# Eight pauses of GpSimd between gathers removed, and three transfers moved from SyncE's queue to ScalarE's, in a two-layer graph kernel

## The chip, the cores and the metric

The kernel runs on one core of a Trainium2 chip. The metric is device time in microseconds, the median of several runs; lower is better. One further execution was taken with the hardware profiler, and all stages, waits and durations below are of that execution, in microseconds from its start.

## The reference

```python
h = maximum(layernorm(x), 0)                       # x: 4096 x 512, adj: 4096 x 4096, all f32
d = rowsum(adj) ** -0.5                            # 0 where the row sum is 0
x = x + relu((d[:, None] * adj * d[None, :]) @ h @ W0 + b0)      # layer 0

h = maximum(layernorm(x), 0)                       # layer 1
s, t = (h @ W1) @ a[:512], (h @ W1) @ a[512:]
e = leaky_relu(s + t.T, 0.2)                       # 4096 x 4096
p = softmax(where(adj > 0, e, -1e12), axis=1)
q = -softmax(where(adj > 0, -e, -1e12), axis=1)
x = x + elu(concat([p @ h, q @ h], axis=1) @ wtrans)
```

About 0.8% of the entries of adj are nonzero (a symmetric random mask with the diagonal).

## The kernel before

Layer 0 is dense: TensorE multiplies the whole adj with the normalized rows. While it runs, the kernel finds, for every block of 64 output rows, which nodes are neighbours of any of them, and writes index lists. Layer 1 is sparse: for each pair of blocks it gathers the rows of h that the pair needs from a table in HBM and works on those alone.

**Tables.** A row of a table holds 512 numbers of h, the score t (column `ROW_T`), and the mask bits of the output rows that the table serves. There are eight tables, each for eight blocks, that is four pairs. `table[4]` (`tab0` = 4) is filled first. Most rows of the other tables are written in layer 0; the last two groups of rows (512 and 256 rows, `GROUPS[-2:]`) are copied from `table[4]` during layer 1 by `copy_rows` (L1350 to L1355, two DMAs of 1032 and 516 KB per table). Table 5, the next one, is copied after the second product of layer 1 in program order, the others every six blocks.

**Gathers.** `gather` (L453 to L464) issues indirect DMAs from GpSimd's queue, one for each list of 128 nodes. A pair has 22 of them in three tiles of 8, 6 and 8 (`CHUNKS`), called a = 0, 1, 2. The first block of a pair uses tiles 0 and 1, the second block tiles 1 and 2, so each block has 14. `gather0` does this for pair 16, whose work is woven into the end of layer 0; `gather1` for pairs 17 to 31 and 0 to 15. The tiles of a pair have one buffer for even and one for odd places k in the order of pairs (`g_pools[k % 2, a]`), so a gather can start when the product two pairs earlier has read its buffer.

**Pauses.** `pause` (L447) is a GpSimd copy of one column of the last gathered part of a tile into a small tile `mark`. GpSimd executes in order, so the gathers behind it are issued only when that tile has landed. There are eight: one in `gather0`, and seven in `gather1`, for (k, a) = (0, 1), (1, 0), and a = 2 with k from 1 to 5. The scheduler of the framework places instructions of an engine by their expected readiness, except those that `tc.keep_in_program_order` ties to each other; the early pauses stand two gathers after the tile that they wait for.

**One block r of layer 1.** `weights(r)`: on VectorE the scores z = s + t (L469) and the slope step (L475), on ScalarE two exponentials, of z and -z (L479), on VectorE two masks for each gathered tile (L488) and a tree of sums (L493 to L499). For the first four blocks, r = 34 to 37 (`first`), scores, exponentials and masks are done for each gathered tile by itself. `product(r)`: 14 matrix products on TensorE (28 records, L1306), then the reciprocal `rl` of the sums (a matmul `cs`, L504, and L506 on VectorE) and the scaling of u to `us` on ScalarE (L1315). `turn(r)`: four transposes (`tp`, L514) and copies to `ut` on ScalarE (L518). `finish1(j)`, for a pair: 8 products with `wt_sb` (16 records, L1329), the elu and the store. The text calls a block's product r34, its tiles p34, z34, us34, and so on. Pair n holds blocks 2n and 2n + 1; g1_18 is tile a = 1 of pair 18.

The loop over blocks is a pipeline: behind product(r) stand the gathers for the pair two further on, the weights of block r + 2 and the turn of block r - 1.

**Transfers by SyncE.** At the start of layer 1, SyncE's queue holds two loads of s, then `wt_sb` (wtrans, 2048 KB), then after the second product the two copies to table 5; after that the loads and stores of the finished pairs.

Of the kernel before, what the change touches and what calls it, by code (L numbers as in the profile page):

```python
# [11 lines left out]
I32 = mybir.dt.int32  # L12
# [7 lines left out]
P = 128  # L20
# [239 lines left out]
def gcn_gat_kernel(  # L260
# [23 lines left out]
    nc = tc.nc  # L284
# [33 lines left out]
    with sbuf(name="init", bufs=1) as init:  # L318
        column = init.tile([P, P], F32, name="column")
        nc.vector.memset(column[:, 0:1], 0.0)  # L320
        n = 1
# [38 lines left out]
    def rows_of(g, e):  # L360
        return table[g][e * ER : e * ER + EN, :].rearrange("(k p) c -> p k c", p=P)
# [80 lines left out]
    def put_row(queue, g, j, h):  # L442
        return queue.dma_start(  # L443
            out=rows_of(g, j // EJ)[:, j % EJ, :ROW_W], in_=h.bitcast(I32)
        )

    def pause(pool, gt):  # L447

        mark = pool.tile([P, 1], I32, tag="mark", name="mark", bufs=1)
        i = nc.gpsimd.tensor_copy(mark, gt[:, gt.shape[1] - 1, 0:1])  # L450
        tc.keep_in_program_order(i)

    def gather(gt, n, a):  # L453

        c = sum(CHUNKS[:a])
        for k in range(CHUNKS[a]):
            nc.gpsimd.indirect_dma_start(  # L457
                out=gt[:, k, :],
                out_offset=None,
                in_=table[2 * n // RPT],  # L460
                in_offset=bass.IndirectOffsetOnAxis(
                    ap=idx[n // NH][:, n % NH, c + k : c + k + 1], axis=0
                ),
            )  # L464

    def scores(s, z, t):

        n = z.shape[1]
        return nc.vector.tensor_tensor(  # L469
            z, t.to_broadcast([P, n, RB]), s.unsqueeze(1).to_broadcast([P, n, RB]), ALU.add  # L470
        )

    def exps(z, p, bound=False, pin=False):

        nc.vector.scalar_tensor_tensor(z, z, ALPHA, z, ALU.mult, ALU.max)  # L475
        if bound:
            nc.vector.tensor_scalar(z, z, 2 * MAXS, -2 * MAXS, ALU.min, ALU.max)
        for g in range(2):
            i = nc.scalar.activation(p[:, :, g, :], z, AF.Exp, scale=(1.0, -1.0)[g])  # L479
            if pin:  # L480
                tc.keep_in_program_order(i)

    def mask_out(r, p, mask):

        m = mask[:, :, r % RPT * RB : (r % RPT + 1) * RB]
        for g in range(2):
            e = p[:, :, g, :]
            nc.vector.scalar_tensor_tensor(e, m, 0.0, e, ALU.is_gt, ALU.mult)  # L488

    def tree(pool, r, q, half, tag="tree", bufs=3):  # L490

        t = pool.tile([P, half, 2 * RB], F32, tag=tag, name=f"tree{r}", bufs=1)
        nc.vector.tensor_tensor(t, q[:, :half], q[:, half : 2 * half], ALU.add)  # L493
        while half > 2:
            n = half // 2
            nc.vector.tensor_tensor(t[:, :n], t[:, :n], t[:, half - n : half], ALU.add)
            half -= n
        total = pool.tile([P, 2 * RB], F32, tag="total", name=f"total{r}", bufs=bufs)
        nc.vector.tensor_tensor(total, t[:, 0], t[:, 1], ALU.add)  # L499
        return total  # L500
# [22 lines left out]
    with sbuf(name="y0", bufs=1) as y_pool, sbuf(name="wa", bufs=1) as wa_pool, sbuf(name="bits", bufs=4) as bits_pool, sbuf(name="small0", bufs=4) as small, ExitStack() as rest, ExitStack() as lists:  # L523
# [403 lines left out]
        i0, n = GROUPS[0]  # L927
        with sbuf(name="w0", bufs=1) as w0_pool, sbuf(name="ain", bufs=9) as ain, sbuf(name="xs", bufs=5) as x_pool, sbuf(name="at6", bufs=5) as at_pool, sbuf(name="bits6", bufs=3) as bits6, sbuf(name="ln", bufs=3) as ln_pool:
# [3 lines left out]
            for g in range(2):  # L932
                nc.gpsimd.dma_start(
                    out=lst_dram[g].rearrange("(p n) o -> p (n o)", p=P), in_=dummy
# [4 lines left out]
            for g in range(NTAB):  # L939
                nc.gpsimd.dma_start(  # L940
                    out=table[g].rearrange("(e r) c -> e r c", r=ER)[:, EN, :], in_=zero[:NE]
# [3 lines left out]
                out=rows_of(tab0, late0 // EJ)[:, late0 % EJ : late0 % EJ + n_late, :],  # L945
                in_=zero.unsqueeze(1).to_broadcast([P, n_late, ROW]),
# [178 lines left out]
        with sbuf(name="work2", bufs=2) as work, sbuf(name="sums2", bufs=2) as sum_pool, sbuf(name="at2", bufs=4) as at_pool, sbuf(name="scratch", bufs=1) as scratch, sbuf(name="pair", bufs=1) as pair:  # L1125
            gts, ps0, totals, u0 = {}, {}, {}, {}
# [6 lines left out]
            def gather0(a):  # L1133
                if a < 2:
                    k = 1 - a
                    gt = y_pool.tile([P, Y_PARTS[k] * F], F32, tag=f"y{k}", name=f"g0_{a}")
                else:
                    gt = t_pool.tile([P, T_PARTS[0] * 3 * H], F32, tag="t0", name=f"g0_{a}")
                gt = gt[:, : CHUNKS[a] * ROW].bitcast(I32)
                gts[a] = gt.rearrange("p (k c) -> p k c", c=ROW)  # L1140
                gather(gts[a], PAIR0, a)
                if a == 2:
                    pause(small, gts[a])

            def parts0(r):
                a = r % 2
# [59 lines left out]
            def step(jp):  # L1206
# [19 lines left out]
            k = late0 % EJ  # L1226
            nc.gpsimd.dma_start(
                out=rows_of(tab0, late0 // EJ)[:, k : k + n_late, ROW_W:],
                in_=late_m[:, k : k + n_late].bitcast(I32),
# [14 lines left out]
    def sparse_layer1():  # L1244
        with ExitStack() as pools:

            def pool(name, bufs):
                return pools.enter_context(sbuf(name=name, bufs=bufs))
# [4 lines left out]
            tmp, small, p_pool = pool("tmp", 1), pool("small1", 2), pool("p", 3)  # L1253
# [3 lines left out]
            wt_sb = wt_pool.tile([P, 2 * FC, F], F32, name="wt_sb")  # L1257
# [3 lines left out]
            def load_s(k):  # L1261

                srow[k] = s_pool.tile([P, 4 * P], F32, tag="s", name=f"s{k}")
                return nc.sync.dma_start(
                    out=srow[k], in_=s_dram[4 * k * P : 4 * (k + 1) * P].partition_broadcast(P)
                )

            def gather1(n, a):
                k = pairs.index(n)
                gt = g_pools[k % 2, a].tile([P, CHUNKS[a], ROW], I32, tag="g", name=f"g{a}_{n}")  # L1270
                gather(gt, n, a)
                gath.setdefault(n, []).append(gt)
                if (k, a) in ((0, 1), (1, 0)) or a == 2 and 0 < k < 6:
                    pause(small, gt)

            def parts(r):

                t = gath[r // 2][r % 2 : r % 2 + 2]
                return (t[0], 0, t[0].shape[1]), (t[1], t[0].shape[1], t[1].shape[1])

            def weights(r):

                nk = sum(CHUNKS[r % 2 : r % 2 + 2])
                z = tmp.tile([P, nk, RB], F32, tag="z", name=f"z{r}", bufs=1)
                p = p_pool.tile([P, nk, 2, RB], F32, tag="p", name=f"p{r}")
                s = srow[r // 8][:, r % 8 * RB : (r % 8 + 1) * RB]
                for gt, k, n in parts(r):
                    scores(s, z[:, k : k + n], gt[:, :, ROW_T : ROW_T + 1].bitcast(F32))
                    if r in first:
                        exps(z[:, k : k + n], p[:, k : k + n])  # L1290
                        mask_out(r, p[:, k : k + n], gt[:, :, ROW_W:].bitcast(U8))
                if r not in first:
                    exps(z, p)
                    for gt, k, n in parts(r):
                        mask_out(r, p[:, k : k + n], gt[:, :, ROW_W:].bitcast(U8))
                wgt[r] = (p, tree(small, r, p.rearrange("p k g c -> p k (g c)"), nk // 2))
# [20 lines left out]
            def turn(r):  # L1317
                if r % 2 == 0:
                    uts[r // 2] = ut_pool.tile([P, 2, FC, P], F32, tag="ut", name=f"ut{r // 2}")
                turn_u(r, us.pop(r), uts[r // 2])  # L1320
# [26 lines left out]
            first = order[:4]  # L1347
            later = [*range(tab0 + 1, NTAB), *range(tab0)]

            def copy_rows(g, j, n):  # L1350

                r = j // EJ * ER + j % EJ * P
                return nc.sync.dma_start(
                    out=table[g][r : r + n * P, :ROW_W], in_=table[tab0][r : r + n * P, :ROW_W]
                )  # L1355

# [2 lines left out]
                tc.keep_in_program_order(load_s(wanted.pop(0)))  # L1359
            for a in range(3):  # L1360
                gather1(pairs[0], a)
            tc.keep_in_program_order(
                nc.sync.dma_start(out=wt_sb, in_=wtrans.rearrange("(c p) f -> p c f", p=P))
            )
            for a in range(3):
                gather1(pairs[1], a)
            weights(order[0])
            weights(order[1])
            for k, r in enumerate(order):
                product(r)  # L1370
                if k % 6 == 1 and k // 6 < len(later):
                    for j, n in GROUPS[-2:]:
                        tc.keep_in_program_order(copy_rows(later[k // 6], j, n))
                if k + 4 - k % 2 < len(order):
                    for a in ((0,), (1, 2))[k % 2]:
                        gather1(order[k + 4 - k % 2] // 2, a)
                if k + 2 < len(order):
                    weights(order[k + 2])
                    if wanted and order[k + 2] % 8 == 7:
                        load_s(wanted.pop(0))  # L1380
                if k:
                    turn(order[k - 1])
                if k == 2:
                    finish1(PAIR0)
                if k % 2 and k > 1:
                    finish1(order[k - 3] // 2)
            turn(order[-1])
            finish1(order[-1] // 2)

    sparse_layer1()  # L1390
    bad = nc.values_load(
        verdict[0:1, 0:1],
# [38 lines left out]
```

## Time and profile before

| | |
|---|---|
| timed runs, us | 2120.07, 2124.37, 2126.74 (median 2124.37) |
| profiled execution, us | 2135.61, its span 2133.8 |
| mean TensorE clock granted | 0.976 of full |
| busy share: PE, DVE, ACT, POOL | 94%, 53%, 24%, 43% |
| end of layer 0's products | about 1038 us |
| first gather of pair 17 | 1052.58 us |
| first product of pair 17 | 1083.57 us |

In the profile, PE is TensorE, PEld its weight loads, DVE VectorE, ACT ScalarE, POOL GpSimd, SP SyncE; SPq and ACTq are their DMA issues. A group's row names the line of the code, the engine, the operation, what it writes and reads, how often it occurs, its busy time and mean duration in ns, and the idle time of the engine just before it with the main releaser. "issue" is idle time for which the profile shows no releaser. A row of the timeline gives start, duration, engine, line, operation and in brackets the idle time before it. A GpSimd gather ends in the profile [...] not when its data have landed.

### The profile page before, as it was taken

The page shows a single profiled execution, that of the slowest core. Times are in us where ns is not written, and L with a number is a line of the kernel's source. Part 1 is how long each engine was busy: PE and PEld are TensorE (multiplying, and loading weights), DVE is VectorE, ACT ScalarE, POOL GpSimd, SP SyncE. Part 2 cuts the span into 40 slices and gives each one's busy share as a digit, 9 for nine tenths or more (in the row PEclk, how much of TensorE's full clock was granted, in tenths as well). Part 3 has the DMA queues.
Part 4 walks back from the last instruction along what each step waited for, and adds up shares of the span by engine and source line. Part 5 has one row for each costly group of instructions (what it writes and reads, how often), then busy time and mean ns, then how long its engine had stood idle before and what let it go on. Part 6 is the DMA issues. An engine that isn't in the chain of part 4 may idle for free.

```text
span 2133.8 us, 20055 instructions
## 1 busy us (share of the span) xinstructions
PE 2010.4 (94%) x6456; PEld 1184.6 (56%) x6456; DVE 1121.2 (53%) x2805; ACT 511.8 (24%) x876; POOL 923.9 (43%) x988
## 2 busy tenths in 40 slices
PE   6999999999898989899878998999999999999998
PEld 3444447888787768787434443444444444444443
DVE  5444526463896469835644435445445445445441
ACT  4645612223232310001111212122122122122120
POOL 2010001111123310322467667777777777677740
PEclk9999999999999999999989999999999999999999
DMA  9988918786977875556587778888888888887850
GB/s 372 372 309 320 365 47 281 266 305 199 344 241 251 260 258 172 169 167 199 164 284 238 241 227 265 262 281 243 276 254 272 248 276 246 239 247 235 239 168 21
DMA packets 188041, 524.12 MB, mean 246 GB/s; under 512 B 25235, under 2 KB 34419, under 8 KB 187926
## 3 DMA queue, kind: packets, MB, share of 16 engines
q0 software_dynamic: 71296, 275.22, 41.7%
q1 hardware_dynamic: 88480, 196.46, 27.1%
q10 hardware_dynamic: 28150, 51.07, 6.7%
q8 instruction: 52, 0.85, 0.2%
q14 instruction: 63, 0.52, 0.1%
HBM read 430.83 MB, written 102.92 MB: 250 GB/s over the span
## 4 chain that ended last, share of the span: by engine, by line
PE 47%; DVE 6%; DMA 4%; POOL 4%; issue 3%; ACT 1%; ACTq 1%; another core or an unknown queue 0%; DVEq 0%; SPq 0%; POOLq 0%
PE u L1306 30%; PE o L1329 10%; PE p L899 5%; POOL g L457 4%; DMA at<-in_adj_t 2%; DMA g<-table,idx 1%; DVE keys L393 1%; PE tp L514 1%; DVE lst L391 1%; DMA table<-h 1%; ACTq L443 1%; PE u L1182 1%; ACT m L722 1%; DVE p L488 0%
## 5 line engine op out<-in xcount | busy, mean ns | idle before, releaser
L457 POOL DMA_INDIRECT g<-table,idx x704 | 753.4, 1070 | 266.6 <-issue 197.6
L1306 PE MATMUL u<-g,p 128*128 128x512 f32 x1736 | 766.7, 598 | 14.9 <-DVE p L488 9.7
L1306 PEld LDWEIGHTS u<-g,p 128*128 128x128 f32 x1736 | 326.8, 191 | 405.5 <-issue 382.2
L469 DVE TENSOR_TENSOR z<-g,s 128x512 f32<-128x512 f32 (+1 forms) x124 | 77.4, 624 | 422.6 <-DMA g<-table,idx 376.0
L899 PE MATMUL p<-t,sums 128*128 128x256 f32 x832 | 249.7, 385 | 15.9 <-DVE sums L887 12.8
L899 PE MATMUL p<-y,sums 128*128 128x256 f32 x832 | 253.6, 387 | 6.3 <-DVE sums L889 5.5
L899 PE MATMUL p<-y,at 128*128 128x256 f32 x832 | 253.9, 387 | 3.9 <-DMA at<-in_adj_t 2.6
L1329 PE MATMUL o<-wt_sb,ut 128*128 128x512 f32 x512 | 230.5, 603 | 0.9 <-ACT ut L518 0.5
L479 ACT ACTIVATE p<-z 128x896 f32<-128x896 f32 (+2 forms) x136 | 116.1, 903 | 313.3 <-DVE z L475 156.7
L899 PEld LDWEIGHTS p<-t,sums 128*128 128x128 f32 x832 | 160.1, 193 | 39.5 <-DVE sums L887 14.0
L899 PEld LDWEIGHTS p<-y,sums 128*128 128x128 f32 x832 | 161.5, 194 | 31.1 <-DVE sums L889 6.3
L899 PEld LDWEIGHTS p<-y,at 128*128 128x128 f32 x832 | 160.1, 194 | 30.9 <-issue 3.4
L858 PE MATMUL acc<-y,at 128*128 128x512 f32 x384 | 174.9, 593 | 2.4 <-ACT y L708 2.4
L488 DVE SCALAR_TENSOR_TENSOR p<-g,p 128x384 f32<-128x384 uint8 (+1 forms) x256 | 143.6, 620 | 60.8 <-ACT p L479 30.4
L733 POOL DMA_DIRECT2D table<-m x71 | 54.3, 766 | 251.9 <-ACT m L722 146.6
L1329 PEld LDWEIGHTS o<-wt_sb,ut 128*128 128x128 f32 x512 | 96.7, 194 | 111.9 <-issue 111.0
L722 ACT ACTIVATE m<-at 128x1024 uint8<-128x1024 f32 (+1 forms) x110 | 105.0, 987 | 181.2 <-DMA at<-in_adj_t 140.2
L899 PE MATMUL p<-t,at 128*128 128x256 f32 x416 | 127.0, 388 | 18.8 <-DVE w L782 17.7
L685 PE MATMUL yp<-w_sb,hx_t 128*128 128x512 f32 x256 | 122.2, 623 | 18.1 <-ACT y L708 15.8
L1315 ACT ACTIVATE us<-u,rl 128x512 f32<-128x512 f32 x62 | 42.5, 686 | 389.4 <-issue 237.8
L858 PEld LDWEIGHTS acc<-y,at 128*128 128x128 f32 x384 | 70.5, 190 | 80.5 <-issue 76.9
L886 DVE TENSOR_TENSOR sums<-at 128x256 f32<-128x256 f32 x104 | 43.3, 416 | 136.4 <-PE p L899 67.3
(183 smaller groups left out, 1720.3 us busy)
## 6 DMA issues: line engine op xcount, KB each, us to landing
at<-in_adj_t SPq DMA_DIRECT2D x136, 512.0 KB
ar<-in_adj SPq DMA_DIRECT2D x128, 512.0 KB
table<-h ACTq DMA_DIRECT2D x182, 258.0 KB
table<-m POOLq DMA_DIRECT2D x55, 256.0 KB
at<-in_adj_t SPq DMA_DIRECT2D x32, 384.0 KB
g<-table,idx POOLq DMA_INDIRECT x704
xr<-in_x SPq DMA_DIRECT2D x32, 256.0 KB
x<-x1d SPq DMA_DIRECT2D x32, 256.0 KB
```

Source lines behind the costliest of these rows:

```text
L457: nc.gpsimd.indirect_dma_start(out=gt[:, k, :], out_offset=None, in_=table[2 * n // RPT], in_offset=bass.IndirectOffsetOnAxis(ap=idx[n // ...
L469: return nc.vector.tensor_tensor(z, t.to_broadcast([P, n, RB]), s.unsqueeze(1).to_broadcast([P, n, RB]), ALU.add)
L479: i = nc.scalar.activation(p[:, :, g, :], z, AF.Exp, scale=(1.0, -1.0)[g])
L488: nc.vector.scalar_tensor_tensor(e, m, 0.0, e, ALU.is_gt, ALU.mult)
L685: nc.tensor.matmul(yp, hx_t[j][:, c * P : (c + 1) * P], w0_sb[:, c, :], start=c == 0, stop=c == FC - 1,)
L722: nc.scalar.activation(m, at, AF.Sign)
L733: nc.gpsimd.dma_start(out=rows_of(t, e)[:, c:, ROW_W + (a - t * TT) * P // 4 : ROW_W + (b - t * TT) * P // 4], in_=masks[i0][:, c:, (a - i ...
L858: nc.tensor.matmul(a, at[:, 0, it * P : (it + 1) * P], y0[j], start=j == 0, stop=j == NJ - 1)
L886: op(t[:, 0], a[:, :, 0, 1], a[:, :, 1, 1], ALU.add)
L899: i = nc.tensor.matmul(out, left[:, x * P : (x + 1) * P], right, start=jp == 0 and first, stop=jp == NP - 1 and (final or not first),)
L1306: nc.tensor.matmul(u, p[:, k0 + k].rearrange("p g c -> p (g c)"), gt[:, k, :F].bitcast(F32), start=k0 + k == 0, stop=k0 + k == nk - 1,)
L1329: nc.tensor.matmul(po, ut[:, g, c, :], wt_sb[:, g * FC + c, :], start=g == 0 and c == 0, stop=g == 1 and c == FC - 1,)
```

## The change

The function `pause` and its eight calls go. The exponentials of the first four blocks are tied into the program's order (`pin=True`), so that what is tied behind them stays behind them. `wt_sb` is loaded from ScalarE's queue after the weights of the first two blocks, and the two copies to table 5 are issued from ScalarE's queue as well; all later copies stay with SyncE.

```diff
-    def pause(pool, gt):
-
-        mark = pool.tile([P, 1], I32, tag="mark", name="mark", bufs=1)
-        i = nc.gpsimd.tensor_copy(mark, gt[:, gt.shape[1] - 1, 0:1])
-        tc.keep_in_program_order(i)
...
                 gather(gts[a], PAIR0, a)
-                if a == 2:
-                    pause(small, gts[a])
...
                 gath.setdefault(n, []).append(gt)
-                if (k, a) in ((0, 1), (1, 0)) or a == 2 and 0 < k < 6:
-                    pause(small, gt)
...
                     if r in first:
-                        exps(z[:, k : k + n], p[:, k : k + n])
+                        exps(z[:, k : k + n], p[:, k : k + n], pin=True)
...
-            def copy_rows(g, j, n):
+            def copy_rows(queue, g, j, n):
...
-                return nc.sync.dma_start(
+                return queue.dma_start(
...
-            tc.keep_in_program_order(
-                nc.sync.dma_start(out=wt_sb, in_=wtrans.rearrange("(c p) f -> p c f", p=P))
-            )
             for a in range(3):
                 gather1(pairs[1], a)
             weights(order[0])
             weights(order[1])
+
+            tc.keep_in_program_order(
+                nc.scalar.dma_start(out=wt_sb, in_=wtrans.rearrange("(c p) f -> p c f", p=P))
+            )
             for k, r in enumerate(order):
                 product(r)
                 if k % 6 == 1 and k // 6 < len(later):
                     for j, n in GROUPS[-2:]:
-                        tc.keep_in_program_order(copy_rows(later[k // 6], j, n))
+                        queue = nc.scalar if k == 1 else nc.sync
+                        tc.keep_in_program_order(copy_rows(queue, later[k // 6], j, n))
```

In the program as built, the order of the instructions on TensorE is the same in both versions. On GpSimd only the eight copies are gone. On SyncE only the three transfers are gone. On ScalarE and VectorE the order changes around blocks 34 to 38: the load of `wt_sb` follows p35's exponentials; us34 now precedes p36's first exponentials; us35 and, behind it, the copies to table 5 precede p37's exponentials; on VectorE the masks of p36 and of p37 stand behind the scores of their block's second tile, and rl35 stands behind z37's second tile and ahead of the masks of p37.

## The prediction

> **What bounds the kernel now.** I read the page's groups first, then busy time by stage, then the waits of PE and POOL inside the stage that the change touches, then the instructions in order of time there.
>
> ```profile
> L457 POOL DMA_INDIRECT g<-table,idx x704 | 753.4, 1070 | 266.6 <-issue 197.6
> L1306 PE MATMUL u<-g,p 128*128 128x512 f32 x1736 | 766.7, 598 | 14.9 <-DVE p L488 9.7
> ```
>
> Busy time by stage (us from the span's start; length; busy PE, PEld, DVE, ACT, POOL; PE clock; DMA share; GB/s):
>
> ```profile
> 1083.57:1302.90 219.33, 203.00 (x503) 92.62 (x503) 101.62 (x190) 40.71 (x70) 155.21 (x148) 0.96 0.80 242
> 1323.00:2000.00 677.00, 677.00 (x1765) 313.03 (x1764) 333.26 (x617) 139.05 (x232) 496.12 (x466) 1.00 0.83 257
> ```
>
> From 1323 us on PE is never idle: layer 1 is then bound by TensorE, about 31.5 us for a pair of blocks. Only its first seven pairs (1083.57 to 1302.90) leave PE idle, 219.33 - 203.00 = 16.3 us. Whatever this change gains must come from there, or from the 9.7 us just before it. The waits in that stage (in total, times, longest):
>
> ```profile
> PE tp L514 <- ACT us L1315: 11.1, 3, 4.6
> PE tp L514 <- issue: 4.0, 2, 2.3
> POOL mark L450 <- DMA g<-table,idx: 19.0, 7, 5.2
> ```
>
> PE waits for `us`, ACT's scaling of u; `us` stands in order behind exponentials, and its factor `rl` behind a `z` on DVE. Both wait for gathered rows. POOL, which makes the gathers, is meanwhile never held by a buffer (0.3 us on PE in this stage, against 47.0 us, 32 times, from 1320 to 2000 us). So here the chain is POOL, landing, DVE, ACT, PE. One of the waits removed, in order of time on POOL:
>
> ```profile
> 1218.35 0.94 POOL L457 DMA_INDIRECT g<-table,idx  x1 [0.30 <-issue]
> 1224.48 0.69 POOL L450 COPY mark<-g 128x1 int32<-128x1 int32 x1 [5.19 <-DMA g<-table,idx]
> 1225.33 1.78 POOL L457 DMA_INDIRECT g<-table,idx  x1 [0.16 <-DVE z L469]
> ```
>
> POOL ends a gather at 1219.29 and begins the next at 1225.33, where the ordinary gap is 0.30.
>
> [...] from 1084 to 1088 us POOL's queue held 58.9% of the engines' time and SP's 44.9%. [...] here landing follows the end of issue by 3.2 to 5.5 us, and those are the values I use. [...] an output product (16 `o` matmuls) takes 7.03 us warm, but 9.06, 8.31 and 8.73 us after the three waits.
>
> **Part 1: eight pauses go.** The one in layer 0 frees 0.7 us, but six gathers later POOL stands at L1227 for a landing anyway (3.73 us): worth nothing. The other seven, each as the time from the end of the gather before to the start of the next less 0.30:
>
> 3.05 (at 1089.85), 2.79 (1101.90), 1.34 (1123.49), 1.25 (1155.80), 4.10 (1188.57), 5.74 (1224.48), 5.55 (1260.91): 23.8 us in all.
>
> So gathers come earlier by 5.8 us for pair 18's last tiles, 7.2 for pair 19's, 8.4 for pair 20's, 12.5 for pair 21's, 18.3 for pair 22's, 23.8 for pair 23's. No other work hides behind them on POOL. With no drain at the pause, the copy traffic may lengthen landings; from 1262 us on gathers already run without pauses at a DMA share of 0.83, and landings stay covered.
>
> **Part 2: wtrans and the first copies leave SP.** On SP they were issued at 1072.6 to 1077.3 and ran to about 1094, in the landing of the first pair's gathers. In windows of 4 us SP's queue took 75.3% of the engines from 1076 to 1080. The first pair's first gathers, issued by 1073.2, were used only at 1080.10, 6.9 us later instead of about 3.3:
>
> ```profile
> 1080.10 0.69 DVE L469 TENSOR_TENSOR z<-g,s 128x512 f32<-128x512 f32 x1 [4.23 <-DMA g<-table,idx]
> ```
>
> Moved away, this lands near 1076.6, and r34 (the first product, 1083.57) starts about 3.5 us earlier. SP has nothing queued behind the three transfers until 1156.71, so SP gains nothing else.
>
> On ACT three issues are added: 0.38 us for wt_sb, twice 0.61 (the median for such copies) for table 5; together 1.6 us, with slack. By the built program's order wt_sb follows p35's exponentials, so about 1096 us; its first use is the output product after r36, about 1124. The 3.7 MB of wt_sb and copies together took 21 us before, so 28 us for 2.1 MB covers it. The copies stand behind us35, hence behind rl35, which DVE now holds behind z37's second half (pair 18's last gather, landing 1117.7 to 1119): they go out near 1121. A later set of copies (1220.4) was through in under 10 us, so table 5 is ready at 1131 to 1136; POOL wants it for pair 20 at 1152.72 - 7.2 = 1145.5. The cover is about 10 us; beyond it each us would hold POOL.
>
> **Part 3: pinned exponentials change the order on DVE and ACT.** In the built program p36's masks for its first gathered tile now come after z36's second half, which waits for g1_18. That lands at 1112.5 - 5.8 + 2.2 (wt_sb's traffic, as the g1_17 landing took 5.5 us against 3.3) = 1108.9. After z, its slope step and two masks, r36 starts near 1111.4, against 1110.93 now. So the 3.5 us of part 2 are lost again. In return us35 is no longer behind p37's exponentials: the stall at 1123 (4.58 us, then 2.03 us of cold `o`) goes, and r37 ends near 1143.3 instead of 1149.7, 6.4 earlier.
>
> **The sum.** After r37 PE again follows gathers, now pair 20's: rl37, rl38 and us38 wait for g0_20 and g1_20, earlier by 8.4 us, so r40 ends 8.4 to 9 us earlier. From pair 21 on the gathers lead PE by more each pair (12.5, 18.3, 23.8), and the later idle goes: 0.45 + 3.34 + 2.26 = 6.0 us, with 1.70 us of cold `o` and 0.6 at 1301. Total 8.7 + 8.3 = 17 us. From both sides: no more than all idle plus cold work, 16.3 + 5.0 + 2.4 (r34's cold start) + the 3.5, about 27; no less than 8 if landings lengthen by 3 us each and the later idle half stays. Behind, PE is full and nothing is won or lost.
>
> The profiled execution took 2135.61 us (span 2133.8), 11 more than the median of the timed runs, 2124.37. It has two stretches (1021 to 1028 and 1303 to 1323 us) where PE crawls with "issue" as the only cause, some 10 us that I take to be of that execution and leave as they are. Against its own time I expect 2118.6 us; carried to the median, **2107.4 us**.
>
> **Rivals.**
> - *Landings take the pauses' place* (15%). If the DMA engines set the pace, a freed POOL only makes a longer queue, and `z` waits as before. For: share 0.80 with PE idle, and 30 us of POOL work a pair (22 gathers of 1.06 us and gaps of 0.30) against 31.5 of PE leaves little. Against: 356 to 411 GB/s moved from 1076 to 1088, 242 on average. It gives 4 to 9 us, about 2118.
> - *The edit does nothing that counts* (7%): the stalls that go come back as waits of PE for `us` through DVE's order; 2122 to 2127.
> - *Slower: POOL is held by the copies* (10%). Table 5 is issued some 48 us later than now. If these copies need more than 24 us from 1121, because gathers no longer pause for them, pair 20's gathers stall. They lose the 7.2 us gained so far at 31 us and break even with the later pauses at about 24 + 18 = 42 us; at 55 us the loss is 13 us, 2137. Against: the 3.7 MB before took 21 us among gathers.
> - *All idle goes* (8%): 22 to 26 us, 2100.
>
> **How the numbers follow.** The likeliest case (60%) is 2107, by itself 2102 to 2114. To leave out no more than 2 in 10, the range runs from 2099 (all idle) to 2124. About 0.3%, 6.4 us, is what a measurement of this kernel can tell from no change. Faster: 0.60 + 0.08 + most of the first rival, 0.10, 0.78. Same: 0.05 + 0.07 = 0.12. Slower 0.10.
>
> **What would show it.** Right: no `mark` on POOL; gathers of pair 21 start about 12 us earlier against r34's start; `z` at about 1077 for the first pair; PE's waits for `us` under 4 us in the seven pairs; wt_sb and table 5 landed before their use; PE full from about 1200 us. Wrong: POOL waiting on "DMA table<-table" before pair 20; landings more than 6 us after issue through the stage; an `o` product waiting for wt_sb; or idle PE of 15 us or more in those pairs.

## The result and the profile after

| | before | after |
|---|---|---|
| timed runs, us | 2120.07 to 2126.74, median 2123.81 (4) | 2098.72 to 2107.48, median 2104.20 (4) |
| profiled execution, us (span) | 2135.61 (2133.8) | 2098.72 (2096.8) |
| first gather of pair 17, us | 1052.58 | 1049.76 |
| first product of pair 17 (r34), us | 1083.57 | 1078.52 |

The ratio is 0.9901 [0.9875, 0.9928]: 19.6 us faster at the median. The profiled executions differ by 37 us, nearly twice that. The one before was 12 us above its median and the one after is the lowest of its four, so the two traces may not simply be subtracted; the experiments below say what the surplus is.

The groups of the page after, the same two as before:

```profile
L451 POOL DMA_INDIRECT g<-table,idx x704 | 747.8, 1062 | 259.9 <-issue 186.4
L1296 PE MATMUL u<-g,p 128*128 128x512 f32 x1736 | 762.4, 596 | 9.8 <-DVE p L482 9.8
```

A gather costs POOL what it did (1062 ns against 1070): the time that went is not in the work. Busy time by stage after, in windows with the same meaning, from r34 on (us from the span's start; length; busy PE, PEld, DVE, ACT, POOL; PE clock; DMA share; GB/s):

```profile
1078.52:1287.71 209.19, 208.28 (x536) 95.97 (x537) 107.54 (x201) 43.62 (x75) 162.89 (x153) 0.99 0.88 281
1287.71:1965.00 677.29, 677.29 (x1769) 313.40 (x1768) 336.57 (x623) 139.73 (x235) 496.99 (x469) 1.00 0.84 259
```

PE is idle for 209.19 - 208.28 = 0.9 us where it was idle for 16.3. The DMA share rises from 0.80 to 0.88, as the same rows arrive in less time. The later window is full in both. PE's waits of the stage, all of them (total, times, longest), and what is left in front of the gathers:

```profile
PE u L1296 <- DVE p L482: 9.8, 2, 9.5
PE tp L508 <- ACT us L1305: 0.6, 1, 0.6
...
POOL g L451 <- issue: 45.4, 149, 0.3
```

The 11.1 us of waits for `us` are 0.6. Of the 9.8 us at the first line 9.5 stand ahead of r34, outside the window. On POOL every gap is the ordinary 0.30; no `mark` is left. The first pair's last scores, in order of time, and r34:

```profile
1075.05 0.69 DVE L463 TENSOR_TENSOR z<-g,s 128x512 f32<-128x512 f32 x1 [5.83 <-DMA g<-table,idx]
...
1078.52 1.22 PE L1296 MATMUL u<-g,p 128*128 128x512 f32 x1 [9.47 <-DVE p L482]
```

DVE now waits 5.83 us here instead of 4.23, yet ends earlier: a longer wait at one place can be the sign of work that came forward.

### The profile page after: what moved, and what is told of

Same layout as the page of the kernel before. It is cut to its first block, busy times and chain, and to the rows that moved or that the text cites. A ratio compares the mean times of both kernels' runs of the same rounds, so it can differ in the third digit from the quotient of the medians.

```text
span 2096.8 us, 20037 instructions
## 1 busy us (share of the span) xinstructions
PE 1996.2 (95%) x6456; PEld 1180.1 (56%) x6456; DVE 1120.1 (53%) x2805; ACT 511.3 (24%) x876; POOL 917.0 (44%) x980
## 3 DMA queue, kind: packets, MB, share of 16 engines
q1 hardware_dynamic: 86640, 192.78, 27.1%
## 4 chain that ended last, share of the span: by engine, by line
PE 49%; DVE 6%; DMA 5%; POOL 3%; issue 2%; ACTq 1%; ACT 0%; DVEq 0%; SPq 0%; POOLq 0%
PE u L1296 32%; PE o L1319 10%; PE p L893 5%; POOL g L451 3%; DMA g<-table,idx 2%; DVE keys L393 1%; PE tp L508 1%; DVE lst L391 1%; DMA table<-h 1%; DMA ld<-li,off 1%; DMA at<-in_adj_t 1%; PE u L1174 1%; ACTq L443 1%; DVE prod L816 0%; DMA table<-m 0%
## 5 line engine op out<-in xcount | busy, mean ns | idle before, releaser
L451 POOL DMA_INDIRECT g<-table,idx x704 | 747.8, 1062 | 259.9 <-issue 186.4
L463 DVE TENSOR_TENSOR z<-g,s 128x512 f32<-128x512 f32 (+1 forms) x124 | 77.5, 625 | 390.4 <-DMA g<-table,idx 357.8
L1319 PE MATMUL o<-wt_sb,ut 128*128 128x512 f32 x512 | 225.1, 592 | 0.5 <-ACT ut L512 0.5
L893 PEld LDWEIGHTS p<-t,sums 128*128 128x128 f32 x832 | 159.6, 193 | 37.5 <-DVE sums L881 15.5
L893 PEld LDWEIGHTS p<-y,sums 128*128 128x128 f32 x832 | 160.7, 193 | 29.9 <-DVE sums L883 7.3
L482 DVE SCALAR_TENSOR_TENSOR p<-g,p 128x384 f32<-128x384 uint8 (+1 forms) x256 | 143.2, 620 | 63.3 <-ACT p L473 62.3
L413 POOL DMA_INDIRECT ld<-li,off x48 | 43.2, 901 | 159.8 <-DMA ld<-li,off 115.8
```

Source lines behind the costliest of these rows:

```text
L413: return nc.gpsimd.indirect_dma_start(out=lst_dram[g][:, :], out_offset=bass.IndirectOffsetOnAxis(ap=off[g][:, e, c : c + 1], axis=0), in_ ...
L451: nc.gpsimd.indirect_dma_start(out=gt[:, k, :], out_offset=None, in_=table[2 * n // RPT], in_offset=bass.IndirectOffsetOnAxis(ap=idx[n // ...
L463: return nc.vector.tensor_tensor(z, t.to_broadcast([P, n, RB]), s.unsqueeze(1).to_broadcast([P, n, RB]), ALU.add)
L893: i = nc.tensor.matmul(out, left[:, x * P : (x + 1) * P], right, start=jp == 0 and first, stop=jp == NP - 1 and (final or not first),)
L1319: nc.tensor.matmul(po, ut[:, g, c, :], wt_sb[:, g * FC + c, :], start=g == 0 and c == 0, stop=g == 1 and c == FC - 1,)
```

## The experiments

**Theories.** A: the pauses give the whole gain; they kept gathers, and through `z`, `rl` and `us` the products, late. Rival: the gain comes with the transfers that leave SP. What stayed open after the first four runs was a second thing, called the crawl here: stretches in which PE executes one instruction in 0.7 to 2.8 us with no releaser. The traces before had them, the trace after had none.

All runs in one table. The ratio is to the kernel before, run between them on the same chip: e1 to e4 on one (2144.55 us), e5 to e8 on a second (2146.64), e9 to e11 on a third (2145.52), e12 on a fourth (2124.37). "r34" to "r46" are starts of products and "end" is PE's last instruction, each less the start of pair 17's first gather, worked out from the traces. "Issue" is PE's idle time without a named releaser from 1000 to 1350 us, and "crawl" what is left of it without the gaps that are waits, as told below the table. "us" are PE's waits for `us` or `ut` from r34 to 1350 us, the unnamed ones among them.

| run | us | ratio, interval | r34 | r36 | r37 | r40 | r46 | end | issue | crawl | us |
|---|---|---|---|---|---|---|---|---|---|---|---|
| before | 2123.81 | 1 | 31.0 | 58.4 | 85.0 | 144.0 | 250.3 | 1073.1 | 17.1 | 8.4 | 15.1 |
| after | 2104.20 | 0.9901 [0.9875, 0.9928] | 28.8 | 56.4 | 76.0 | 128.6 | 225.3 | 1039.0 | 0 | 0 | 0.6 |
| e1_pauses_gone | 2132.85 | 0.9945 [0.9931, 0.9960] | 30.9 | 58.1 | 100.5 | 152.4 | 249.1 | 1062.8 | 26.3 | 21.5 | 4.6 |
| e2_transfers_moved | 2141.83 | 0.9996 [0.9977, 1.0015] | 27.9 | 62.3 | 84.8 | 141.7 | 256.2 | 1073.5 | 27.4 | 9.3 | 12.1 |
| e3_early_pauses | 2136.96 | 0.9969 [0.9956, 0.9983] | 28.0 | 62.5 | 84.3 | 144.2 | 251.0 | 1064.7 | 27.1 | 13.8 | 5.9 |
| e4_late_pauses | 2140.72 | 0.9979 [0.9963, 0.9994] | 27.9 | 59.8 | 100.4 | 152.3 | 248.9 | 1066.4 | 30.6 | 21.5 | 0 |
| e5_after_again | 2132.36 | 0.9939 [0.9919, 0.9960] | 28.1 | 59.5 | 95.7 | 147.6 | 244.3 | 1059.9 | 27.1 | 19.2 | 0 |
| e6_tiles_placed | 2135.48 | 0.9950 [0.9931, 0.9969] | 27.9 | 56.1 | 99.1 | 151.0 | 254.4 | 1068.1 | 24.0 | 22.8 | 0.2 |
| e7_copies_later | 2140.68 | 0.9976 [0.9966, 0.9986] | 28.4 | 59.6 | 94.9 | 153.4 | 250.1 | 1068.5 | 28.2 | 23.4 | 0 |
| e8_before_again | 2150.61 | one run | 29.9 | 58.9 | 87.3 | 143.2 | 249.5 | 1076.6 | 25.9 | 13.1 | 16.3 |
| e9_tail_pauses | 2132.96 | 0.9946 [0.9924, 0.9968] | 28.3 | 59.4 | 96.5 | 148.4 | 245.1 | 1058.9 | 18.6 | 10.4 | 0 |
| e10_pauses_on | 2153.40 | 1.0038 [1.0025, 1.0051] | 30.3 | 58.7 | 86.5 | 142.5 | 250.7 | 1083.0 | 16.1 | 7.1 | 16.5 |
| e11_light_breaks | 2128.98 | 0.9926 [0.9901, 0.9952] | 27.9 | 60.9 | 82.2 | 149.1 | 245.8 | 1059.5 | 22.0 | 14.2 | 0 |
| e12_both_breaks | 2109.97 | 0.9931 [0.9917, 0.9944] | 28.7 | 57.9 | 77.5 | 132.2 | 228.9 | 1042.6 | 0 | 0 | 2.4 |

Not every gap without a named releaser is crawl. Two waits for `us` in the trace before, each with the row of ScalarE that made this `us`:

```profile
1127.07 0.69 ACT L1315 ACTIVATE us<-u,rl 128x512 f32<-128x512 f32 x1 [0.44 <-DVE rl L507]
1127.81 1.11 PE L514 MATMUL tp<-ident,us 128*128 128x128 f32 x4 [4.58 <-ACT us L1315]
...
1170.51 0.69 ACT L1315 ACTIVATE us<-u,rl 128x512 f32<-128x512 f32 x1 [9.80 <-DVE rl L507]
1171.25 0.66 PE L514 MATMUL tp<-ident,us 128*128 128x128 f32 x4 [1.74 <-issue]
```

Both times PE starts 0.74 us after `us` began, 0.05 us after it ended; the view names the releaser only once. A gap is counted here as a wait if a `us`, mask or sum that the instruction reads ended 50 to 60 ns before it, as at nearly all gaps with a named releaser (52 to 56 ns). Most of the long single gaps are such waits. So counted, the kernels with all the pauses of layer 1 (before, e2, e8, e10) have 12 to 17 us of waits for `us`, those with none of them 0 to 5. The 4.6 us of e1 lie inside a crawl and end 0.6 us after `ut`.

### e1: the pauses alone

The kernel before without `pause` and its calls; the transfers stay with SP, `exps` without `pin`.

```diff
-                if a == 2:
-                    pause(small, gts[a])
...
-                if (k, a) in ((0, 1), (1, 0)) or a == 2 and 0 < k < 6:
-                    pause(small, gt)
```

> The kernel before without the eight pauses; wtrans and the first copies stay on SyncE's queue, nothing is pinned. Theory A (PE is held by POOL's gathers in the first seven pairs, so the pauses cost the time): nearly the whole gain, 0.991 to 0.994 of before (13 to 19 us); r34 starts as late after the first gather of pair 17 as before (31 us), and PE waits under 5 us from there to pair 23. Rival B (the transfers in the first pair's landing cost the time, and POOL would be held by landings anyway): 0.998 to 1.001.

Measured 0.9945, just outside what theory A expected, and the same as the whole change on such a chip (e5, 0.9939; the intervals cover each other). The pauses give the gain.

### e2: the rest alone

The changed kernel with `pause` and all eight calls put back.

```diff
...
+                if (k, a) in ((0, 1), (1, 0)) or a == 2 and 0 < k < 6:
+                    pause(small, gt)
```

> The changed kernel with all eight pauses put back: only the pinned exponentials and the move of wtrans and the first copies to ScalarE's queue are left. Theory A: r34 starts 2 to 4 us earlier against the first gather of pair 17, but from r38 on PE follows the same paused gathers as before, so 0.997 to 1.001 of before. Rival B: most of the gain, 0.990 to 0.994.

Measured 0.9996 [0.9977, 1.0015]: no change, as theory A has it; the rival falls. The columns r34 and r36 show why. With the transfers on SP (before, e1, e8, e10) r34 starts 29.9 to 31.0 us after the first gather, in all others 27.9 to 28.8: the move does bring the first product forward by 2 us or so. At r36 the four stand at 58.1 to 58.9 and the others at 56.1 to 62.5, median 59.5: it is gone again. In e2 PE waits 6.3 us for masks ahead of r36, where the kernel before waits 4.58 us for `us` behind it. The run takes the moved transfers and the pinned order together; it does not separate the two.

### e3 and e4: which pauses

The changed kernel with four early pauses back (e3), or with the three late ones (e4). In the profile before, these cost POOL 3.05 + 2.79 + 1.34 + 1.25 = 8.4 us and 4.10 + 5.74 + 5.55 = 15.4 us.

```diff
...
+                if (k, a) in ((0, 1), (1, 0), (1, 2), (2, 2)):
+                    pause(small, gt)
```
```diff
...
+                if a == 2 and 2 < k < 6:
+                    pause(small, gt)
```

> The changed kernel with four pauses put back, those of (k, a) = (0, 1), (1, 0), (1, 2) and (2, 2); before, they took 8.4 us of POOL. Theory A with one account of lead (a delay of POOL costs only what the lead of the gathers over PE does not cover): here there is no lead yet, so 5 to 8 us slower than the changed kernel, 0.993 to 0.995 of before. If every us of pause counted alike (17 to 25 us for 23.8 us of pauses), these four would cost 6 to 9 us, so it is the next run that tells the two apart.

> The changed kernel with three pauses put back, a = 2 with k = 3, 4 and 5; before, they took 15.4 us of POOL. One account of lead: in the changed kernel the masks of r40 to r45 are ready 12 to 16 us before PE wants them, so the 15.4 us are covered but for 3 us at most: the same as the changed kernel, 0.989 to 0.992 of before. If every us of pause counted alike: 11 to 15 us slower than the changed kernel, 0.995 to 0.997.

Measured 0.9969 and 0.9979; e3 too lies a little above what theory A gave it. Against 0.9942, the mean of e1 and e5, the early pauses cost 0.0027 (5.8 us), the late ones 0.0037 (7.9 us), all of them 0.0054 (11.6 us). So by the timed runs neither group is free, and the time of e4 falls clearly outside the reading in which an account of lead, once filled, pays for later pauses. It doesn't follow that each us counts alike either (11 to 15 us were expected of e4 then): 15.4 us of late pauses cost little more than 8.4 us of early ones. With intervals of 0.0015 either way these two numbers carry no more than that. (In their own traces the pauses took 8.8 us of POOL in e3 and 13.8 in e4.)

Where the time went, the traces tell only for e3: from r37 to r40 PE takes 59.9 us there and 51.9 in e4 and e5, and waits for `us` are back. In e4 the stretch from r37 to r46, in which all three pauses lie, takes 148.5 us as in e5 (148.6), with no wait for `us`. In that execution, 4.9 us below its median, the late pauses were covered by the lead of the gathers. What the timed runs of e4 lost is not shown.

### e5 and e8: both kernels again, for the crawl

Unchanged kernels.

> The changed kernel once more, beside the kernel before. Theory A (the gain is idle PE of the first seven pairs, won by earlier gathers): ratio 0.988 to 0.993, that is 15 to 25 us; less than the pauses alone (0.9945) would mean that the moved transfers cost something. On the crawl (stretches in which PE runs one instruction in 0.7 to 2 us with no releaser): if it belongs to something that the change removed, this profile has again under 3 us of such idle PE from 900 to 1330 us; if it is of the execution and not of the kernel, it has 15 to 30 us, as every other profile had.

> The kernel before once more, for its profile. If the crawl belongs to places of the program, it stands again at 1022 to 1027 and 1294 to 1319 us and nowhere else; if it is of the execution, its place or length differs by several us.

The changed kernel gave 0.9939 [0.9919, 0.9960], 14.3 us, just outside the 0.988 to 0.993 expected; the interval overlaps with the first one. Its profile now has the crawl, 19.2 us of it, so the crawl does not belong to what the change removed. In order of time on PE in e5, inside r36 (start, duration, then the idle time before it in brackets):

```profile
1126.46 0.59 PE L1296 MATMUL u<-g,p 128*128 128x512 f32 x1 [0.19 <-issue]
...
1128.57 0.59 PE L1296 MATMUL u<-g,p 128*128 128x512 f32 x1 [1.51 <-issue]
...
1131.37 1.01 PE L1296 MATMUL u<-g,p 128*128 128x512 f32 x1 [2.21 <-issue]
...
1132.79 1.01 PE L1296 MATMUL u<-g,p 128*128 128x512 f32 x1 [0.42 <-issue]
```

Starts lie 2.11, 2.80 and 1.42 us apart where the ordinary distance is 0.43, and the durations of 1.01 came at a lowered clock (0.54 in the window from 1130 to 1140; in the trace before, such a matmul takes 0.59 us at 1.00, from 1098 to 1110, and 1.06 at 0.50, from 1083 to 1087). All 28 records of r36 are there, so nothing is hidden in the gaps. The lowered clock is not where the crawl starts: from 1119 to 1130 us, with the first gaps, the granted clock was 1.00. PE's waits of the stage in e5 (1090 to 1290 us), and in e8 (1085 to 1345):

```profile
PE u L1296 <- issue: 14.2, 11, 3.4
PE u L1296 <- DVE p L482: 6.6, 1, 6.6
```
```profile
PE tp L514 <- issue: 13.4, 8, 3.3
PE u L1306 <- DVE p L488: 9.6, 2, 8.4
PE tp L514 <- ACT us L1315: 8.6, 2, 5.8
```

The waits for `us` are there with the pauses (8.6, and 7.7 more under "issue") and gone without them, as in the first two profiles. Of the 14.2 us of e5, 3.4 are a wait for masks ahead of r36. The crawl is there in both, but it is not equally long: 13.1 us in e8, 19.2 in e5. Both have it in layer 0's last products; the stretch in layer 1 has another place, 1324 to 1337 in e8 and 1126 to 1145 in e5. (The single gap of 4.5 us that both have at about 1083 is pair 16's wait for `us`.) So the crawl does not explain why e5 is the faster of the two; if anything, it hides a part of the gain.

### e6: tiles in another order

The changed kernel with its buffers for gathered rows made in another order; with it the first gathers of pair 17 go out in the order a = 1, 0, 2 instead of 2, 0, 1, and p36's masks no longer stand behind z36's second tile.

```diff
-            slots = ((0, 0), (1, 0), (1, 2), (1, 1), (0, 1), (0, 2))
+            slots = ((0, 0), (1, 0), (1, 2), (1, 1), (0, 2), (0, 1))
```

> The changed kernel with the first pair's gathers and the scores ordered tile by tile, so that p36's masks for its first tile no longer stand behind z36's second half. If the first product waits for landing and score order: it starts about 4 us earlier after the first gather (24 to 26 us instead of 28.8), r36 ends about 5 us earlier, and the time is 4 to 6 us below the changed kernel (ratio to before 0.986 to 0.991). Rival: PE is then held by the next tile's landing, the gain is gone by r36 and the time is that of the changed kernel within 2 us.

0.9950, not faster than the changed kernel. r34 started at 27.9 us, as everywhere, not at 24 to 26: the first half of the expectation is wrong. r36 did start 3.4 us earlier than in e5 (56.1 against 59.5), but r37 came later, since a crawl of 16.7 us lay in between. On time the rival is the nearer one (2135.48 us against 2132.36 in e5, the intervals overlap); its reason, a gain gone by r36, is not what the trace shows.

### e7: is the cover of the copies real?

The copies to table 5 issued behind us36 instead of us35.

```diff
-                if k % 6 == 1 and k // 6 < len(later):
+                if k == 2 or k > 1 and k % 6 == 1 and k // 6 < len(later):
...
-                        queue = nc.scalar if k == 1 else nc.sync
+                        queue = nc.scalar if k == 2 else nc.sync
```

> The changed kernel with the copies to table 5 issued one block later from ScalarE, behind us36, about 1134 us instead of 1113. The cover between the end of that traffic and the first gather of pair 20 was about 11 us. If that cover is real and the transfer takes 13 to 15 us: GpSimd waits 8 to 10 us on the copies ahead of pair 20's first gather, of which PE feels 0 to 3 us because the gathers by then lead PE by 8 to 12 us: ratio 1.000 to 1.002 against the changed kernel. Rival (no lead to spend): PE loses 8 to 10 us, 0.004 to 0.005 slower than the changed kernel.

Measured 0.9976 [0.9966, 0.9986], 0.0037 or 8 us slower than the changed kernel on that chip: near the rival's 0.004 to 0.005. The copies went out at 1161.2, not 1134, because us36 itself was late, behind a crawl (1145 to 1159); their packets ran from 1162.6 to 1168.0. POOL in order of time:

```profile
1155.17 0.95 POOL L451 DMA_INDIRECT g<-table,idx  x1 [0.30 <-issue]
1169.30 1.05 POOL L451 DMA_INDIRECT g<-table,idx  x1 [13.19 <-DVE total L493]
```

The gather at 1169.30 is the first of pair 20, the first that reads table 5. The row names DVE as releaser, because a sum there ended last before it; what ended 1.3 us ahead are the copies' last packets. This is the mechanism of the prediction's slower rival, and its price: 13 us of POOL, 8 us of time.

### e9, e10 and e11: when does the crawl start, and when does it end?

Theory B in these expectations is that a long run of gathers without a stop starts the crawl and that the end of the run ends it. In the profiles it begins 17 to 23 us into such a run in layer 0 (the one pause of the kernels before, under 1 us, taken as no stop) and 27 to 55 us into it in layer 1, and it ends within some 5 us of the run's end. In layer 1 that end says little, since GpSimd stops there for buffers that PE holds (in e5 12.6 us, 6 times, from 1050 to 1345 us); in layer 0 GpSimd stops at the end of its lists, at 1028.4 us in the trace before, whatever PE does. e9 is the changed kernel with draining pauses in `gather0`; e10 is the kernel before with pauses for three pairs more; e11 is the changed kernel with breaks that read the tile before, and so do not wait for the 6 or 8 gathers just issued.

```diff
...
                 gather(gts[a], PAIR0, a)
+                pause(small, gts[a])
```
```diff
-                if (k, a) in ((0, 1), (1, 0)) or a == 2 and 0 < k < 6:
+                if (k, a) in ((0, 1), (1, 0)) or a == 2 and 0 < k < 9:
```
```diff
...
+                if len(gts) > 1:
+                    pause(small, [*gts.values()][-2])
...
+                if a and k < 9:
+                    pause(small, gath[n][a - 1])
```

> The changed kernel with three pauses in layer 0's last gathers (pair 16), one behind each of its three tiles, two or three gathers later, so that no run of gathers there is longer than about 10. Theory B (the crawl of PE is started by a long unbroken run of gathers and ends when GpSimd stops): the first crawl, 2 to 10 us of idle PE between 1020 and 1042 us in every profile but one, is gone; the crawls of layer 1 stay; the time is 3 to 9 us below the changed kernel, ratio to before 0.990 to 0.9925. Rival (the crawl has another cause): it stands there still, and the time is that of the changed kernel, 0.994, or up to 4 us more because pair 17's gathers start later.

> The kernel before with its pauses of GpSimd going on for three pairs more, behind the last tiles of the pairs at k = 6, 7 and 8. Theory B: the crawl that follows the last pause (8 us of idle PE between 1294 and 1337 in both profiles of the kernel before) does not come there; it comes after the new last pause, about 1400 us, or not at all, since by then GpSimd stops for buffers. Its price is 3 times 4 to 5 us of GpSimd, of which PE feels part. Time within 6 us of the kernel before. Rival (the crawl belongs to its place in the program, whatever the gathers do): it stays at 1294 to 1337, and the time is 5 to 12 us longer.

> The changed kernel with small breaks: behind each tile of gathers, in pair 16 and in pairs 17 to 25, GpSimd reads one column of the tile before it, which has nearly always landed by then, so that a break costs about 1 us and leaves 6 to 8 gathers in flight. If a mere break in the run of gathers is enough against the crawl: idle PE without a releaser from 1000 to 1350 us falls from 24 to 30 us to under 8, and the time is 10 to 20 us below the changed kernel (ratio to before 0.985 to 0.989). If only a drained queue helps, or the crawl has another cause: 20 us or more of such idle time, and the time is 0 to 8 us above the changed kernel (0.994 to 0.998), for some 15 breaks of 1 us.

The place went as theory B has it, three times on one chip. In e9, layer 0's last products (1015 to 1045 us) have no wait without a releaser; the first line is PE's only wait there, the second one of the pauses:

```profile
PE p L899 <- DVE sums L887: 4.4, 1, 4.4
```
```profile
1016.72 0.19 POOL L450 COPY mark<-g 128x1 int32<-128x1 int32 x1 [3.84 <-DMA g<-table,idx]
```

In e11 the breaks don't wait there, and the crawl is in the same place as ever (2.3 of the 8.1 us are a wait for a sum):

```profile
PE p L899 <- issue: 8.1, 8, 2.3
```
```profile
1020.20 0.19 POOL L450 COPY mark<-g 128x1 int32<-128x1 int32 x1
```

So a mere instruction between the gathers didn't stop it in e11, and three pauses, the first of 3.8 us, kept it away in e9. The one pause in layer 0 of the kernels before, 0.6 to 0.8 us of wait for a landing, did not: before, e2, e8 and e10 have the crawl around it. In e10 no crawl is left from 1280 to 1340, where the kernel before has 5.7 and 8.0 us in its two profiles; the only wait there is one for `us`. It comes at 1408 to 1423 instead, 38 us behind the new last pause (1370.4), and ends when POOL stops at 1421:

```profile
PE tp L514 <- ACT us L1315: 2.5, 1, 2.5
```
```profile
1408.44 1.30 PE L1329 MATMUL o<-wt_sb,ut 128*128 128x512 f32 x2 [0.77 <-issue]
1411.26 0.62 PE L1329 MATMUL o<-wt_sb,ut 128*128 128x512 f32 x1 [1.53 <-issue]
```

The time didn't follow. e9 lost the 8 us of crawl in layer 0 and is as fast as e5 (0.9946 against 0.9939); e11 (0.9926) cannot be told from it and lies in neither of its two expectations; e10 pays 8 us for its pauses, more than the 6 that theory B allowed. Less crawl is not less time as long as another wait takes the place.

### e12: both kinds of break

```diff
...
+                pause(small, gts[a])
...
+                if a and k < 9:
+                    pause(small, gath[n][a - 1])
```

> The changed kernel with the three draining pauses in layer 0's last gathers and the small breaks of about 1 us behind the tiles of pairs 17 to 25. If what each did to the crawl is kept: no idle PE without a releaser from 1015 to 1045 us, at most 10 us of it from 1090 to 1350 us, and the time 4 to 9 us below the changed kernel (ratio to before 0.990 to 0.992). Rival: the idle time only changes its name, because PE then waits for gathered rows instead; ratio 0.993 to 0.996, no faster than the changed kernel.

There is no crawl at all in this profile. But this chip ran the kernel before in 2124.37 us, 21 less than the other three, and the changed kernel had no crawl in its first profile either, without any break; so whether the breaks or the chip did it is open. The ratio is 0.9931 [0.9917, 0.9944]; beside the 0.9901 of the change alone, where the kernel before took 2123.81, it is no gain, and it lies where the rival had it. No run was measurably faster than the changed kernel.

## Why the prediction was right

**What held.** The forecast was 17 us and 2107.4 us, measured 19.6 and 2104.2. What bounds the stage, the chain POOL, landing, DVE, ACT, PE, was read rightly: the waits for `us` go with the pauses (e5, e8 and the last column of the table), the rest of the change gives nothing by itself (e2), and from about 1200 us PE is full. The output products that were slow behind these waits (in the trace before the granted clock was 0.50 there, from 1127.8 to 1132, 1187.4 to 1190 and 1260 to 1262 us) all take 7.03 us in the trace after, at 1.00. The split of the sum, 8.7 us by the early pauses and 8.3 by the late ones, fits the 5.8 and 7.9 that e3 and e4 charge for them, within what these can tell; for the late ones no trace shows it. The forecast of 17 lies between the 19.6 of the first comparison and the 14.3 of e5; that it came so near is in part luck, since terms of its sum were off both ways, as told below.

**Part 1.** Pair 21's gathers start 90.2 us after r34, 15.5 earlier than before (105.7); 12 was expected. The surplus of 3.7 us arises in the first pair, where pair 18's first gather follows pair 17's by 28.4 us instead of 32.1. In the trace before POOL waited there 3.22 us for `ut`, which was late: VectorE began pair 16's last `rl` 3.19 us after the recorded end of its `cs`, in the trace after 0.11 us. (It is 2.7 to 4.3 us in the 12 profiles with a crawl and 0.11 in the two without.) This wait was not in the sum. Landings stayed at a median of 4.2 to 5.3 us from the start of issue, 8.2 at most, so they did not take the pauses' place, as the rival had it.

**Part 2.** Expected: r34 3.5 us earlier. Measured: 2.2 against the first gather, and 2.3 in the mean of all runs of either kind. The load of `wt_sb` was issued at 1089.01 and through by 1106, 13 us ahead of its first use. The copies went out here:

```profile
1113.24 1.42 ACTq L1343 DMA_DIRECT2D table<-table  x2
```

They were through by 1128, and POOL wanted the table at 1138.71: cover 11 us, predicted 10. e7 shows what lies beyond it. That the change of queue has no value by itself was the author's estimate; e2 agrees as far as it goes: the move and the pinned order together gave 0.9996.

**Part 3, the step that was off.** r36 was to wait some 4 us for z36's second tile and start 31.3 us behind r34; it started 27.6 behind and waited 0.35, because its last gather had landed by 1103.7 where 1108.9 was reckoned. So the 2.2 us won at r34 were kept in this execution, and r37 gained 9.1 us instead of 6.4. In the other runs with moved transfers, the loss at r36 is there, on average nearly as predicted (32.1 us behind r34, e6 apart). The term that was mis-sized most is the one behind it: r40 gained 15.4 us in the profile against 8.4 to 9. Pair 20's first gather came 11.1 us earlier after the first one (89.0 against 100.1) instead of 7.2, 3.7 of it the wait of POOL above. And r40 gained more than these gathers did, so it no longer followed them: PE was full already, and the later idle of the stage had nothing left to take.

**The crawl.** "Some 10 us that I take to be of that execution" was right about its size and in that the change does not remove it (e5); but it is no matter of a single execution, since 12 of 14 profiles have it. The two stretches hold 7.6 us of idle PE, but the instructions between the gaps are slower too: r46 alone took 21.4 us where an undisturbed product takes 12.3. The two profiles differ by 2.8 us up to pair 17's first gather, 25.0 from there to r46 and 9.1 behind it, together the 37 us. The last part is r46's crawl, and the first may be that of layer 0; they make up 11.9 of the 17 us by which the profiles differ beyond the timed 19.6. The 25.0 us contain 0.7 us of crawl (1301 to 1303) and the 3.7 us above. The rival "all idle goes" describes that one profile; the medians lie with the likeliest case.

**Slower.** The rival's mechanism exists: in e7 the copies held POOL for 13.2 us. It didn't come up in the changed kernel because there they took 15 us from 1113, not the 24 us from 1121 that it needs.

## What to carry to other kernels

A wait on an engine that only feeds others is worth what the consumer lacks, not what the waiting engine loses: 23.8 us of pauses gave 12 to 20 us. When two profiles differ by more than their medians, count the idle time without a named releaser in both before any of it is put down to the change, and take out first the gaps that end just behind a result which the instruction reads: those are waits, 8.7 of 17.1 us in the trace before. And where a transfer is moved later, measure the cover in front of its reader: 11 us were left here, and one block later they were gone.

## What the runs showed of the hardware

PE fell into a crawl, one instruction in multiples of about 0.7 us (starts 1.42, 2.11 and 2.80 us apart in e5), 17 to 55 us into a run of indirect gathers by GpSimd, in 12 of 14 profiles, and came out of it within some 5 us of the end of the gathers. It began at a granted clock of 1.00 (e5, 1119 to 1130 us). With three pauses that waited 3.84, 0.95 and 3.18 us for landings it stayed away from layer 0 (e9), and with pauses for three pairs more it came 38 us behind the last of them (e10); a pause with 0.6 to 0.8 us of wait (before, e2, e8, e10) and breaks without a landing (e11) didn't keep it away. Two profiles had long runs of gathers and no crawl (after, with no gap above 0.77 us from 1049.8 to 1441.4 us, and e12), and past 1350 us, where every profile has 11 to 21 runs of 28 us or more, only e10's first one shows more than 3 us of it. So a long run is needed, as far as seen, but not enough. The cause of the crawl is open. The three chips on which every profile had a crawl, of 7 to 23 us, ran the kernel before in 2144.6 to 2146.6 us, the other two in 2123.8 and 2124.4.
